# An attention and mixture-of-experts layer: query tiles loaded over sixteen units in place of the last three, and two shared-expert results kept in SBUF

## The chip, the cores and the metric

The kernel runs on one core of a Trainium2 chip. The metric is the device time of one execution in microseconds (us), as the median of several runs. Engines are written as the profile has them: PE (TensorE, matrix products), PEld (its weight loads), DVE (VectorE), ACT (ScalarE), POOL (GpSimd) and SP (SyncE, which here only issues DMAs). "SPq" and "POOLq" are the instruction queues of SP and POOL.

## The reference

The input x is 4 batches of 2048 tokens of 256 numbers. Two halves follow each other, each with a layernorm before and after and an added residual.

```python
x = x + _layernorm(attn(_layernorm(x)))
x = x + _layernorm(ffn(_layernorm(x)))
```

The attention has 16 heads of 16 numbers. Each head projects a token's query and key to one number (q_proj, k_proj), and a query i gathers the values v_j with a triangular weight (the reference does so by sorting and prefix sums):

```
out_i = sum_j max(0, 1 - |q_i - k_j| / b_h) * v_j / 2048
```

The feed-forward part has one shared expert for every token (512 hidden numbers, scaled by a sigmoid gate) and 64 routed experts. It works on all 8192 tokens at once: each token goes to the 8 experts with the largest softmax probability, an expert keeps its first 128 rows, and the results, weighted, are added to the shared expert's:

```python
w, idx = jax.lax.top_k(probs, TOP_K)          # TOP_K = 8, of 64
y = out_e[e_flat, slot] * w_flat[:, None]     # experts' rows, weighted
y = jnp.where((pos < CAPACITY)[:, None], y, 0)   # CAPACITY = 128
return y.reshape(T, TOP_K, H).sum(axis=1) + shared
```

## The kernel before

**The attention loop** takes most of the time. It has 1024 units, 256 for each batch. A unit is one head and one key tile of 128 keys, against all 2048 queries of the batch. Units come in phases of 64: 16 key tiles s, and for each of them the phase's 4 heads j. So a unit is written (s, j), and the last key tile's units are (15, 0) to (15, 3).

`score(t)` forms the weights of unit t in a tile `hat` of 128 x 2048 numbers. ScalarE computes |q - k| from the head's query tile `qb` (line 1558; for some units VectorE does it in two instructions, lines 1553 and 1555), and VectorE cuts it to the triangle in place (line 1562). `product(t)` (line 1588) multiplies on PE with the values, in four pieces of 512 queries that belong to the units t, t-1, t-2 and t-3. Only when the last piece is issued, three units later, is the hat tile given back.

`load_q(n)` (line 1539) loads the query tile of head n: one number for each query, broadcast over the 128 partitions, in two DMAs, 512 KB in SBUF. Query tiles, hat tiles and a few others share 13 large buffers, handed out strictly in turn: `take` pops the buffer that was given back longest ago, `give` appends one. A query tile is given back when its head's last score (s = 15) has read it. For the next phase's four heads the kernel calls `load_q` at (11, 0), (15, 0), (15, 1) and (15, 2). A load waits on SP until its buffer is free, and all other DMAs that SP issues wait behind it.

**Background work.** All else (projections, layernorms, shared expert, routing, routed experts) is a list of tasks in a planner, `Background`. A task names its engine, a cost, the tasks it depends on, and buffers that it takes and gives back: "slot" (10 tiles of 128 x 1024), "big" (the 13 large ones), "bank" (PSUM) and "v". Every unit calls `step()`, which emits the tasks whose turn has come by the planner's own clock (costs, the lags between engines, and a task's `lat` where it has one). The plan is made when the kernel is built, so it fixes each engine's order; on the chip an engine waits wherever the data isn't there. After the loop `drain()` plans the rest, the tail, in the same way.

**The feed-forward part by halves.** Tokens are counted in 16 chunks of 512, four for each batch. Chunks 0 to 7 (batches 0 and 1) have their experts' sums early. For batches 2 and 3 the routed experts are worked through in the tail as 15 items. An item gathers its rows (`L1217`, POOL), has its products on PE (`L1229`, `L1240`), scales them on VectorE (`L1254`) and adds them into `y_d` in memory by an indirect accumulating DMA, the scatter (`L1258`, POOL). Item i gathers only after item i-5 has scattered. There are two such targets, `y_d[1]` and `y_d[2]` for the two halves of a pair of experts; a token's result is the sum of both and of the shared expert.

The shared expert's results of batch 2 (`shared(c)` in `finish`) are stored into `y_d[1]` (line 619), so that the scatters add onto them, and once more into a second tensor, `ysh_d` (line 624), for a seldom-taken repeat at the end, which isn't run with these inputs. All scatters wait for all of these stores (`ys = stored[2]`). The shared results of batch 3 stay in SBUF.

**The final stage.** `final(c)` forms a chunk's output: a load of 512 KB from `y_d` (line 1281), for chunks 8 to 15 a second load and an add on VectorE (line 1288); for chunks 12 to 15 an add of the shared rows from SBUF (`more`, line 1314); then the layernorm: statistics (1292), means and variances (1296, 1297), a power of -1/2 on POOL (1298), shift (1301, 1302), scaling on ScalarE (1307). Last, an accumulating DMA adds the rows to the output tensor in memory (1321, POOL), where the attention's result already lies. Chunks 0 to 7 run beside the items; 8 to 15 wait for the last scatter.

**Zeros.** `y_d[2]` and batch 3's part of `y_d[1]` are set to zero by twelve stores of 512 KB from one large buffer of zeros, every eight units of batch 1 (lines 1649 to 1657).

Of the kernel before, what the change touches and what calls it, by code (L numbers as in the profile page):

```python
# [11 lines left out]
ALU = mybir.AluOpType  # L12
# [128 lines left out]
def sandwich_kernel(ctx: ExitStack, tc: tile.TileContext, x_in, wqT, bq, wkT, bk, wvT, bv, wprojT, log_bw,  # L141
                    gate_w, sgate_w, sgu_w, sd_w, egu_w, ed_w, out):
    nc = tc.nc
    P = 128
    B, T, F = x_in.shape
# [3 lines left out]
    NT = T // P  # L149
    CH = 4  # L150
    NCH = NT // CH
    CT = CH * P
# [28 lines left out]
    NE = 2  # L181
# [4 lines left out]
    ysh_d = dram.tile([T, F], F32, name="ysh_d")  # L186
# [10 lines left out]
    def yrows(r0, n, j=0):  # L197

        p, r = part(r0)
        return rows(y_d[p + j], r, n)  # L200
# [22 lines left out]
    def rows(ap, r0, n):  # L223
        return ap[r0:r0 + n * P, :].rearrange("(n p) f -> p n f", p=P)

    with ExitStack() as ph:
# [14 lines left out]
        def make(tag):  # L241
# [12 lines left out]
                return bigp.tile([P, T], F32, tag=tag, name=f"{tag}_{uid[0]}")  # L254
            return ps.tile([P, BK], F32, tag=tag, name=f"{tag}_{uid[0]}")

        NES, ess = 4, []
        bg = Background(make)
        bg.free["slot"] = [(f"s{i}", 0) for i in range(NSLOT)]
# [73 lines left out]
        def chunkview(t_):  # L333
            return t_[:, :CH * F].rearrange("p (n f) -> p n f", n=CH)
# [121 lines left out]
        def finish(b, after=()):  # L456

            env = {}
# [102 lines left out]
            def shared(c):  # L561
# [32 lines left out]
                for i2 in range(2):  # L594
# [15 lines left out]
                    if i2 == 0:  # L610
# [5 lines left out]
                    a = bg.add("pe", 1.07, lambda f=mmy: f(3), [a], put=acts if i2 == 1 else [], env=env)  # L616
                    yy += [e0, bg.add("dve", 0.45, lambda f=evy: f(1), [a, e0], put=[py], env=env)]
                free_act = a
                free_ys = bg.add("sp", 1.0, lambda ys=ys, r0=r0: nc.sync.dma_start(yrows(r0, CH, 0),
                                                                                   chunkview(env[ys])),  # L620
                                 yy, put=[] if b == NE else [ys], env=env)
# [645 lines left out]
        def final(env, c, deps, more=None, xd=(), tag=""):  # L1267


            yy, sm, xx = ("yy" + tag, c), ("sm" + tag, c), ("xx" + tag, c)  # L1270
            r0 = c * CT
            two = c >= NE * NCH
            S = lambda o, n: env[sm][:, o:o + n]
            st = lambda i: S(i * 6, 6)
            mv = lambda: S(CH * 6, 2 * CH).rearrange("p (n a) -> p n a", a=2)
            rs, sh = lambda: S(CH * 8, CH), lambda: S(CH * 9, CH)
            yv = lambda i: env[yy][:, i * CH * F:(i + 1) * CH * F]
            y3 = lambda: yv(0).rearrange("p (n f) -> p n f", n=CH)

            def load(i):  # L1280
                nc.sync.dma_start(yv(i).rearrange("p (n f) -> p n f", n=CH), yrows(r0, CH, i))
            l0 = l1 = bg.add("sp", 1.0, lambda: load(0), deps, get={yy: "big" if two else "slot"}, env=env)
            if two:
                l1 = bg.add("sp", 1.0, lambda: load(1), [l0])
            put = [yy]

            def add():
                nc.vector.tensor_tensor(yv(0), yv(0), yv(1), ALU.add)

            def stats():  # L1290
                for i in range(CH):
                    nc.vector.bn_stats(st(i), y3()[:, i, :])

            def scale():
                for i in range(CH):
                    nc.vector.bn_aggr(mv()[:, i, :], st(i))
                nc.vector.tensor_scalar_add(rs(), mv()[:, :, 1], EPS)
                nc.gpsimd.tensor_tensor(out=rs(), in0=rs(), in1=mhalf, op=ALU.pow)  # L1298

            def shift():  # L1300
                nc.vector.tensor_tensor(sh(), mv()[:, :, 0], rs(), ALU.mult)
                nc.vector.scalar_tensor_tensor(out=sh(), in0=sh(), scalar=-1.0, in1=cv[:, c * CH:(c + 1) * CH],
                                               op0=ALU.mult, op1=ALU.subtract)

            def norm():
                for i in range(CH):
                    nc.scalar.activation(y3()[:, i, :], y3()[:, i, :], AF.Identity, bias=sh()[:, i:i + 1],  # L1307
                                         scale=rs()[:, i:i + 1])
            a = bg.add("dve", 0.0, lambda: None, [l0, l1], get={sm: "v"}, env=env)
            put.append(sm)  # L1310
            if two:
                a = bg.add("dve", 1.25, add, [a])
            if more is not None:
                a = bg.add("dve", 1.25, lambda: nc.vector.tensor_tensor(yv(0), yv(0), more(), ALU.add),
                           [a] + list(xd))
            a = bg.add("dve", 1.7, stats, [a])
            a = bg.add("dve", 0.7, scale, [a], lat=2)
            a = bg.add("dve", 0.35, shift, [a])
            a = bg.add("act", 2.1, norm, [a])
            if not tag:  # L1320
                return bg.add("pool", 2.0, lambda: nc.gpsimd.dma_start(rows(of, r0, CH), y3(), accum_op=ALU.add), [a],  # L1321
                              put=put, env=env)
            lx = bg.add("sp", 1.0, lambda: nc.sync.dma_start(chunkview(env[xx]), rows(x1_d, r0 - NE * T, CH)), [l1],
                        get={xx: "slot"}, env=env)
            a = bg.add("dve", 1.25, lambda: nc.vector.tensor_tensor(yv(0), yv(0), env[xx][:, :CH * F], ALU.add), [a, lx])
            return bg.add("sp", 1.0, lambda: nc.sync.dma_start(rows(of, r0, CH), y3()), [a], put=put + [xx], env=env)
# [207 lines left out]
        def load_q(n):  # L1534

            b, g, p, s, j, h = unit(n // 4 * UP + n % 4)
            qb[n] = take(f"qb_{b}_{h}")
            for m in range(KF):
                nc.sync.dma_start(qb[n][0][:, m * HK * P:(m + 1) * HK * P],
                                  zq_d[b][m, h:h + 1, :].to_broadcast([P, HK * P]))  # L1540
# [58 lines left out]
        with tc.manual_schedule():  # L1599
            for n in range(4):  # L1600
                load_q(n)
            for t in range(B * NU + 5):
# [46 lines left out]
                if b == 0 and u == 200:  # L1649
                    zt_, z_tag = take("zeros")  # L1650
                    nc.gpsimd.memset(zt_[:, :CH * F], 0.0)
                    zfill = [(1, c) for c in range(NE * NCH, B * NCH)] + [(0, c) for c in range((B - 1) * NCH, B * NCH)]
                if b == 1 and u % 8 == 4 and zfill:
                    i, c = zfill.pop(0)
                    nc.sync.dma_start(yrows(c * CT, CH, i), chunkview(zt_))
# [9 lines left out]
                    bg.flush(last[b + 1]["v"][s:s + 1])  # L1665
                    nc.sync.dma_start(vtile(b + 1, s).rearrange("p a w -> p (a w)"), v_d[b + 1][s])
                if n + 4 < B * H:
                    if s == 11 and j == 0:
                        if ph_ == NU // UP - 1:
                            bg.flush(last[b + 1]["z"])  # L1670
                        if b == 0 and ph_ == 1:
                            bg.flush(last[0])
                        load_q(n + 4)
                    if s == NT - 1 and j < 3:
                        load_q(n + 5 + j)
                was = bg.spent["dve"]
                bg.step()
                spare[0] -= bg.spent["dve"] - was
# [35 lines left out]
            def second(deps, tag):  # L1714
                for c in range(NE * NCH, B * NCH):
                    l = c - (B - 1) * NCH
                    if l < 0:
                        final(env, c, deps, tag=tag)
                    else:
                        final(env, c, deps, lambda l=l: env["ys", l // 2][:, l % 2 * CH * F:(l % 2 + 1) * CH * F],  # L1720
                              outs[2 * l:2 * l + 2], tag)
# [68 lines left out]
```

## Time and profile before

| what | us |
|---|---|
| median of 3 runs | 2340.97 (2337.17 to 2342.14) |
| the profiled execution's own time | 2339.91 |
| its span | 2338.0 |
| ACT busy (84% of the span) | 1966.8 |
| DVE busy (85%) | 1996.1 |
| PE busy (84%) | 1952.5 |
| POOL busy (21%) | 490.4 |
| score on ACT, L1558, 959 x 1.995 | 1837.3 |
| cut on DVE, L1562, 1024 x 1.223 | 1230.3 |
| products on PE, L1588, 8192 x 0.620 | 1115.3 |

The loop's scores start at 64.3 us and end at 2033.6 us; the tail takes the rest. In a group's row the last part is the idle time of the engine just before these instructions, with what ended most of it. In a timeline's row the first two numbers are the start and the length in us, then come engine, line, operation, output and inputs, a count, and in brackets the idle time before it and its releaser. A list of waits gives the total in us, the number of waits and the longest.

### The profile page before, as it was taken

The numbers are of one execution on the slowest core, as the hardware profiler recorded it, in microseconds if no ns is written. First come the engines' busy times: TensorE is split into PE (matmuls) and PEld (weight loads), VectorE is DVE, ScalarE is ACT, GpSimd is POOL, SyncE is SP. The second block draws the span as 40 slices with busy tenths as digits, with TensorE's granted clock in tenths as the row PEclk, the third lists the DMA queues.
The fourth block names the chain that finished last, engine by engine and source line by source line (L and its number), as shares of the span: only waits on it lengthen the run. The fifth ranks groups of instructions, "written<-read, shape, count | busy, mean of one in ns | idle before, by whom it ended". The sixth has DMA issues, their size and how long they took to land. (4 is left out here: it accounts for less than half of the span.)

```text
span 2338.0 us, 32679 instructions
## 1 busy us (share of the span) xinstructions
PE 1952.5 (84%) x12552; PEld 687.2 (29%) x12552; DVE 1996.1 (85%) x3102; ACT 1966.8 (84%) x1269; POOL 490.4 (21%) x339
## 2 busy tenths in 40 slices
PE   7898979888799899677899887878888889987783
PEld 4332323222223222112222222223332223364342
DVE  4799999898999889999989998989999979886335
ACT  2899999898999998999999998989999989742213
POOL 1001010010120000003200003446553234442463
PEclk9999999999999999989999998999999999988897
DMA  4243534427351202142302014465544243355758
GB/s 127 91 133 120 184 103 153 151 88 264 117 162 64 91 19 70 37 147 69 112 19 81 28 54 122 114 186 151 174 121 136 57 134 90 102 177 147 177 124 197
DMA packets 195078, 274.32 MB, mean 117 GB/s; under 512 B 24833, under 2 KB 165505, under 8 KB 194145
## 3 DMA queue, kind: packets, MB, share of 16 engines
q1 hardware_dynamic: 165680, 235.33, 31.2%
q0 software_dynamic: 23824, 31.70, 8.3%
q10 hardware_dynamic: 5408, 5.11, 0.7%
q8 instruction: 101, 1.65, 0.3%
q14 instruction: 65, 0.52, 0.1%
HBM read 189.18 MB, written 82.90 MB: 116 GB/s over the span
## 5 line engine op out<-in xcount | busy, mean ns | idle before, releaser
L1558 ACT ACTIVATE hat<-qb,nk 128x2048 f32<-128x2048 f32 x959 | 1837.3, 1995 | 112.8 <-DMA qb<-zq_d 57.5
L1588 PE MATMUL pa<-hat,v 128*32 128x512 f32 x8192 | 1115.3, 620 | 284.4 <-DVE hat L1562 272.3
L1562 DVE TENSOR_SCALAR hat<-hat 128x2048 f32<-128x2048 f32 x1024 | 1230.3, 1223 | 97.2 <-ACT hat L1558 91.3
L1588 PEld LDWEIGHTS pa<-hat,v 128*32 128x32 f32 x8192 | 186.2, 110 | 900.0 <-DVE hat L1562 652.6
L1066 POOL DMA_INDIRECT y_d<-s,ix x64 | 147.8, 2309 | 286.7 <-DVE s L1064 145.4
L573 PE MATMUL k<-s,sgu 128*128 128x512 f32 x352 | 198.4, 651 | 0.0
L1041 POOL DMA_INDIRECT s<-tab_d,ix x64 | 106.0, 1657 | 327.6 <-DMA qb<-zq_d 259.0
L499 POOL TENSOR_TENSOR rsc<-rsc,mhalf 128x2 f32<-128x2 f32 x24 | 53.4, 2225 | 521.2 <-DVE rsc L498 521.0
L602 PE MATMUL k<-sd,s 128*128 128x256 f32 x384 | 113.7, 428 | 16.9 <-DVE s L589 7.4
L442 PE MATMUL k<-s,s 128*32 128x512 f32 x768 | 102.4, 592 | 0.0
L602 PEld LDWEIGHTS k<-sd,s 128*128 128x128 f32 x384 | 72.2, 205 | 86.4 <-issue 47.8
L573 PEld LDWEIGHTS k<-s,sgu 128*128 128x128 f32 x352 | 54.8, 192 | 136.3 <-issue 121.2
L305 POOL TENSOR_TENSOR rsa<-rsa,mhalf 128x4 f32<-128x4 f32 x16 | 30.8, 1925 | 290.9 <-DVE rsa L304 285.6
L1553 DVE TENSOR_SCALAR hat<-qb,nk 128x2048 f32<-128x2048 f32 x65 | 83.1, 1279 | 0.1
L1555 DVE TENSOR_SCALAR hat<-hat 128x2048 int32<-128x2048 int32 x65 | 79.9, 1229 | 2.2
L350 PE MATMUL k<-h,s 128*128 128x256 f32 x256 | 73.0, 413 | 0.0
L713 DVE MAX8 codes<-scT 128x8 f32<-128x1152 f32 (+2 forms) x48 | 63.4, 1321 | 0.2
L350 PEld LDWEIGHTS k<-h,s 128*128 128x128 f32 x256 | 45.4, 195 | 54.4 <-issue 48.6
L715 DVE MATCH_REPLACE8 scT<-codes,scT 128x1152 f32<-128x1152 f32 (+2 forms) x44 | 57.6, 1310 | 0.0
L607 DVE TENSOR_SCALAR s<-k,gt 128x256 f32<-128x256 f32 x48 | 22.8, 480 | 36.5 <-PE k L602 32.0
L442 PEld LDWEIGHTS k<-s,s 128*32 128x32 f32 x768 | 31.6, 138 | 54.0 <-issue 53.2
L1258 POOL DMA_INDIRECT y_d<-v,ix x28 | 39.9, 1426 | 23.5 <-DMA y_d<-s 7.9
(319 smaller groups left out, 1643.2 us busy)
## 6 DMA issues: line engine op xcount, KB each, us to landing
qb<-zq_d SPq DMA_DIRECT2D x128, 512.0 KB, 5.5
s<-m_d SPq DMA_DIRECT2D x48, 512.0 KB, 4.8
s<-_attn_hidden_states_dram SPq DMA_DIRECT2D x28, 512.0 KB, 5.5
v_d<-h SPq DMA_DIRECT2D x48, 192.0 KB, 2.6
v<-v_d SPq DMA_DIRECT2D x48, 192.0 KB, 2.5
h<-fn_expert_gate_up_w_dram SPq DMA_DIRECT2D x32, 256.0 KB, 3.5
s<-fn_expert_gate_up_w_dram SPq DMA_DIRECT2D x32, 256.0 KB, 2.8
b<-y_d SPq DMA_DIRECT2D x16, 512.0 KB, 9.3
```

Of the source, the lines that this page charges most:

```text
L350: nc.tensor.matmul(env[pk][:, i * F:(i + 1) * F], lhsT=xv[:, k, o:o + P], rhs=wv[:, k, :], start=(k == 0), stop=(k == KF - 1))
L442: nc.tensor.matmul(env[pz][c * CR:(c + 1) * CR, :], lhsT=xv[:, r, :], rhs=env[mp][:, k * 2 * F:(k + 1) * 2 * F], start=(r == 0 and k == 0) ...
L573: nc.tensor.matmul(env[p_], lhsT=sgu[:, k, o:o + P], rhs=featview(env[xT])[:, k, :], start=(k == 0), stop=(k == KF - 1))
L602: nc.tensor.matmul(env[py][:, i * F:(i + 1) * F], lhsT=env[acts[f // 2]][:, o:o + P], rhs=sd[:, f, :], start=(f == 0), stop=(f == NI - 1))
L713: a = bg.add("dve", 1.25, lambda c8=c8: nc.vector.max(out=c8, in_=scT[:, :w]), ev + [a])
L1041: g = bg.add("pool", 1.3, lambda: nc.gpsimd.indirect_dma_start(out=xg(), out_offset=None, in_=tab_d[half][:, :], in_offset=bass.IndirectOf ...
L1066: s = bg.add("pool", 1.9, lambda: nc.gpsimd.indirect_dma_start(out=y_d[half][:, :], out_offset=bass.IndirectOffsetOnAxis(ap=iv(), axis=0), ...
L1553: nc.vector.tensor_scalar(ht, qb[n][0], k, None, ALU.add)
L1555: nc.vector.tensor_scalar(hi, hi, 0x7fffffff, None, ALU.bitwise_and)
L1558: nc.scalar.activation(ht, qb[n][0], AF.Abs, bias=k)
L1562: nc.vector.tensor_scalar(ht, ht, 1.0, 1.0, ALU.min, ALU.subtract)
L1588: nc.tensor.matmul(pa[k, c][32 * j:32 * j + 32, :], lhsT=vt[b, s].rearrange("p a w -> p (a w)")[:, h // 2 * VW + p * D:h // 2 * VW + p * D ...
```

## The change

1. The query tiles of the next phase's heads are loaded at (12, 0), (13, 2), (15, 0) and (15, 1), in place of (11, 0), (15, 0), (15, 1) and (15, 2). Two flushes of the planner that stand with the first load move with it.
2. For chunks 2 and 3 of batch 2 (`LATE`) the shared rows are no longer stored into `y_d[1]`. They are stored into `ysh_d` only, and their slots stay held (`held`) until `final` has added them from SBUF. The scatters therefore wait for the stores of chunks 0 and 1 only. The two parts of `y_d[1]` are set to zero ahead instead: fourteen stores of zeros.
3. In `final`, where shared rows are added from SBUF (chunks 10 to 15 now), the second load becomes an accumulating DMA on POOL onto the first load's tile, which waits until the first has landed, and the add on VectorE goes.
4. The first load of chunks 0 to 7 has a planned latency of 9.

```diff
+        LATE, held = (2, 3), {}
...
+                if b == NE and c in LATE:
+                    held[c] = env, ys, yy
+                    free_ys = bg.add("sp", 1.0, lambda ys=ys, c=c: nc.sync.dma_start(rows(ysh_d, c * CT, CH),
+                                                                                    chunkview(env[ys])), yy)
+                    return
...
-            l0 = l1 = bg.add("sp", 1.0, lambda: load(0), deps, get={yy: "big" if two else "slot"}, env=env)
-            if two:
+            l0 = l1 = bg.add("sp", 1.0, lambda: load(0), deps, get={yy: "big" if two else "slot"}, env=env,
+                             lat=None if two else 9)
+            onto = two and more is not None and not tag
+            if onto:
+                l1 = bg.add("pool", 1.3, lambda: nc.gpsimd.dma_start(y3(), yrows(r0, CH, 1), accum_op=ALU.add), [l0], lat=4)
+            elif two:
                 l1 = bg.add("sp", 1.0, lambda: load(1), [l0])
...
-            if two:
+            if two and not onto:
                 a = bg.add("dve", 1.25, add, [a])
...
-                    zfill = [(1, c) for c in range(NE * NCH, B * NCH)] + [(0, c) for c in range((B - 1) * NCH, B * NCH)]
+                    zfill = [(1, c) for c in range(NE * NCH, B * NCH)] + [(0, c) for c in [NE * NCH + i for i in LATE] + list(range((B - 1) * NCH, B * NCH))]
...
-                    if s == 11 and j == 0:
+                    if s == 12 and j == 0:
...
-                    if s == NT - 1 and j < 3:
-                        load_q(n + 5 + j)
+                    if (s, j) in ((13, 2), (NT - 1, 0), (NT - 1, 1)):
+                        load_q(n + 5 + [(13, 2), (NT - 1, 0), (NT - 1, 1)].index((s, j)))
...
-                    if l < 0:
+                    if l < 0 and c - NE * NCH in held and not tag:
+                        e_, y_, d_ = held[c - NE * NCH]
+                        f_ = final(env, c, deps, lambda e_=e_, y_=y_: e_[y_][:, :CH * F], d_)
+                        bg.add("act", 0.0, lambda: None, [f_], put=[y_], env=e_)
+                    elif l < 0:
                         final(env, c, deps, tag=tag)
```

## The prediction

> **What bounds the kernel now.** First the busy time of the engines by stretches of the span: the 1024 units of the attention loop with what lies ahead of the tail, the tail up to 2204, the stretch of scatters, the final stage.
>
> ```profile
> core 0: us, PE busy (x) PEld busy (x) DVE busy (x) ACT busy (x) POOL busy (x), PEclk, DMA share, GB/s
> 64.00:2034.00 1970.00, 1684.59 (x11323) 525.11 (x11327) 1798.16 (x2415) 1871.45 (x1082) 356.49 (x195) 0.97 0.36 110
> 2034.00:2204.00 170.00, 131.96 (x509) 84.67 (x503) 112.21 (x410) 50.15 (x97) 53.96 (x56) 0.83 0.60 156
> 2204.00:2273.30 69.30, 58.75 (x269) 29.37 (x270) 23.79 (x73) 9.51 (x23) 50.02 (x38) 1.00 0.61 135
> 2273.30:2338.00 64.70, 28.98 (x89) 18.13 (x87) 33.60 (x104) 21.88 (x44) 20.67 (x16) 0.73 0.88 197
> ```
>
> To 2034 ScalarE is busy 95% of the time: its idle time is the loop's loss. The list of what ScalarE waited for says how much there is to win:
>
> ```profile
> ACT hat L1558 <- DMA qb<-zq_d: 57.5, 18, 24.5
> ACT hat L1558 <- PE pa L1588: 49.6, 52, 3.1
> ```
>
> The first line is a late query tile, the second a buffer that a product hadn't given back. Of the 57.5 us, 29.4 (24.5, 1.1 and 3.8) lie at the loop's start, on loads that the change leaves alone; 28.1 are left, in 15 waits. One of them on the timelines of SP and ScalarE, at a phase's end:
>
> ```profile
> 1522.60 3.75 SPq L1539 DMA_DIRECT2D qb<-zq_d  x6
> ...
> 1531.06 2.00 ACT L1558 ACTIVATE hat<-qb,nk 128x2048 f32<-128x2048 f32 x1 [4.64 <-DMA qb<-zq_d]
> 1535.29 2.00 ACT L1558 ACTIVATE hat<-qb,nk 128x2048 f32<-128x2048 f32 x1 [2.06 <-DMA qb<-zq_d]
> 1538.51 3.90 ACT L1558 ACTIVATE hat<-qb,nk 128x2048 f32<-128x2048 f32 x2 [1.22 <-DMA qb<-zq_d]
> ```
>
> Three tiles (six DMAs) are asked for at 1522.6, 1523.6 and 1524.5 and land at 1531.1, 1535.3 and 1538.5: a burst, each tile some 3.7 us behind the last.
>
> After 2204 the work hangs on POOL and SP. POOL's and SP's timelines:
>
> ```profile
> 2163.48 0.46 SPq L619 DMA_DIRECT2D y_d<-s  x1
> 2167.21 1.02 POOL L1298 TENSOR_TENSOR v<-v,mhalf 128x4 f32<-128x4 f32 x1 [10.02 <-DVE v L1297]
> 2200.98 0.36 SPq L619 DMA_DIRECT2D y_d<-s  x1
> 2204.55 1.65 POOL L1258 DMA_INDIRECT y_d<-v,ix  x1 [7.89 <-DMA y_d<-s]
> ...
> 2271.87 1.40 POOL L1258 DMA_INDIRECT y_d<-v,ix  x1 [0.30 <-issue]
> 2273.32 27.26 SPq L1281 DMA_DIRECT2D b<-y_d  x16
> ```
>
> No scatter of the last experts starts until the store of shared chunk 3 (2200.98) has landed; the 28 scatters then run nearly back to back, and the 16 loads of the final stage start at once behind the last. In that stage a chunk's square root on POOL (L1298) comes 5.46 us after the one before (2288.39 to 2321.15, six steps), and DMA is the other limit:
>
> ```profile
> q0 software_dynamic: 4304, 4.26, 45.6%
> q1 hardware_dynamic: 8448, 8.39, 41.5%
> ```
>
> These are the queues of the window 2273 to 2338 (packets, MB, share of 16 engines). q0 is eight accumulating output stores: 0.456 x 65 / 8 = 3.7 us of all engines for 512 KB. q1 is 16 plain loads: 0.415 x 65 / 16 = 1.7 us each.
>
> **The change part by part.** The sum is made against the profiled execution, 2339.91 us (span 2338.0 and 1.9 around it), 1.06 under the median.
>
> *Query loads.* A unit takes 1970/1024 = 1.92 us. Head 1's load moves from the last key tile to six units earlier, 11.5 us: more than its longest wait (4.6), so its waits go (5.95 us over the loop). Head 2's goes one unit up and has one load less ahead of it in the burst: 1.9 + 3.2 us (usual spacing of a burst). Head 3's is issued one unit earlier, but its buffer comes from a product at about the time that the old one did, so only the shorter burst helps: 3 to 5 us. In the phase shown, without stalls the tiles would be wanted at 1526.4, 1528.4 and 1530.4, so they are 4.6, 6.9 and 8.1 us late; after, 0, 1.8 and at most 3.0 to 5, so 3 to 5 of its 7.9 us stay. This is the worst phase; in the others the sums are 1 to 5.5 us and nearly all goes. I take -21 of 28.1; ends 0 (SP still waits for the buffer) and -28. The first load, to key tile 12 from 11, keeps four key tiles of 7.7 us: no price against the slowest landing, 12.7 us. What hides it is the 16 units; without them it costs 3 us a phase.
>
> *Buffers.* All large tiles share 13 buffers, handed out in turn. The earlier load holds one from key tile 13 to 15, so more scores take a buffer that a product gave back only just before. From ScalarE's timeline, the distance in units between the two: today 394 scores at distance 6 (1.9 us of waits for the product), 395 at 5 (12.7), 77 at 4 (11.7; 0.151 each), 39 at 3 (20.3; 0.52 each). Played through with the new order: 424 at 6, 311 at 5, 102 at 4, 54 at 3, six at 2 (no row; 1 us each, twice the row of 3). That is 2.1 + 10.0 + 15.4 + 28.1 + 6 = 61.6 against 46.6: +15. Part of today's waits are themselves followed by query stalls that vanish, so ScalarE runs closer on the products: not under 0 all the same, as no score gets an earlier buffer in those units; the upper end, all lateness of the products shifted by one unit, +17.5. Taken +13. VectorE and PE (85% and 84%) follow in the shadow of ScalarE, with unchanged orders.
>
> *Zero stores.* Two more stores of 512 KB in batch 1, at a DMA share of 0.36 and off any path; the zeros' buffer is held 16 units longer, at most 16 x 0.12 = 2 us of buffer waits. Taken 0; the cover is the idle 64% of DMA, and without it each costs its 1.7 us.
>
> *Late shared rows.* The two stores of batch 2's chunks 2 and 3 into the scatter's target go; the scatters wait only for chunks 0 and 1 (stored by 2082). The two slots stay held up to the end: the orders of PE, VectorE, ScalarE and POOL are the same up to 2156, so this costs nothing in the loop. In the new order POOL's first scatter stands behind the square root at 2167.21, so it can start at 2168, not 2204.55; behind it are now four square roots and their output stores (waits of ScalarE and VectorE) that came before, and they hold the scatters up. Its operand is the bound above: the first expert product (L1254) comes at 2188.96 today. POOL's own work: 28 x (1.40 + 0.30) + 10 x 1.31 = 61 us, in the 68.7 that the stretch takes; with 13 us of square roots and stores in between, from 2168: 2242; from 2190, with half of those: 2258; plus today's 7.5 of waits, 2250 to 2265. PE sets another floor: 89 us of matmuls between 2156.7 and the last scatter, so not before 2246. Taken 2257 for 2273: -16; ends -27 and 0.
>
> *Final stage.* Six of eight chunks lose an add on VectorE (L1288, 1.23 us), but six need the add of the shared rows (L1314) in its place, two of them newly. Today one add is already in the shadow of the square root and L1314 is not; after, L1314 takes the shadow, and the chain is 4.7 us a chunk: 6 x 0.76 = -4.6. Against it six plain loads (1.7 us each) become accumulating DMAs on POOL, each waiting for its first load to land. If one costs the 3.7 us of an accumulating store: 6 x 2.0 = +12 of 16-engine time, a stage of 10 x 1.7 + 14 x 3.7 = 69 for 56.6, which at 64.7 us leaves little room; if it costs a plain load's, 0. Their issue is 1.32 us each on POOL (L1321), which has 5.46 - 1.6 - 1.3 = 2.5 us free per chunk. Taken: nearer to the store (the same queue, the same size), +8; with the adds +3. Ends -5 and +12.
>
> Sum: -21 + 13 - 16 + 3 = -21; 2339.91 - 21 + 1.06 = **2320 us**.
>
> A rule that speaks against it: the Trainium skill, SBUF — State Buffer, section "SBUF: two separate sides", says that GpSimd can't write a DMA's descriptors while VectorE runs certain two-port operations, and (under "A bandwidth-pool intuition that's wrong") gives 620 ns alone against 3100 ns for such a DMA. By that factor of five each accumulate would take 6.6 us of POOL and the time would be 2348, an estimate from that page. The rows bear out less: see the fourth rival.
>
> **The rivals.**
> *The scatters gain little.* Their rows come from experts whose weights and products are themselves late: the last products (L1254) are at 2265.5 and 2268.1, 4 us ahead of the last scatters. If PE's pace and not POOL's decided, the end of the scatters moves 6 us, and the stage loses its +6: -8 - 6 + 6, **2333**. For it: PE 58.75 of 69.3 us; against: product buffers are freed by the scatters, so PE's pace follows POOL's.
> *The loads stay late.* The buffers, not the issue, set when tiles land: main loop +6 (0 to -9 for the loads, +15), tail -13: **2334**. For it: distances fall to 2 just where loads are issued. Against: in the burst shown the issues are 1 us apart and the landings 4.
> *Slower: the accumulates become the bound.* If they go one after another at x us, the stage is 10 x 1.7 + 14x + 9 of lead. The gains ahead of it are 24 us, so it decides from a stage over 65 + 24 + 4.7 = 94, x = 4.9. At the shortest landing of such a store, 5.7 us: 106 us, +41, **2358**. For it: 14 such DMAs in one queue, each but eight behind a load; against: today eight overlap at 3.7, with landings of 8.5.
> *POOL's issue is held out by VectorE.* An indirect DMA's issue takes 2.31 us in the loop (L1066), 1.40 in the tail (L1258). At the worst row, 3.41: 1.6 + 1.3 + 3.4 = 6.3 us a chunk, over 5.46: +5, and the -4.6 is lost: **2330**. Against: output stores take 1.29 to 1.40 us in the stage itself.
>
> **How the numbers follow.** Forecast 0.50 (own range 2304 to 2330); scatters gain little 0.17; loads late 0.10; slower 0.18; POOL held out 0.05. A measurement of this kernel tells 0.2% (4.7 us) from no change. Forecast 0.48 faster, 0.02 same; the second and third 0.19 faster, 0.07 same, 0.01 slower; slower 0.18; the last 0.05 faster: **0.72, 0.09, 0.19**. Range **2302 to 2348**: it leaves out most of the slower case and little below.
>
> **What would show it.** Waits of L1558 for qb near 36 us in all; for PE near 63; hats ending 8 us earlier than 2034; the first L1258 before 2190 and the last by 2262 with no wait for y_d<-s; the final stage 62 to 72 us, ten L1281 loads, q0 over half of the DMA time. Wrong: PE waits over 75, or scatters ending past 2270, or POOL waiting on its own queue's accumulates in the final stage.

## The result

The changed kernel takes 2319.91 us (median of 4 runs, 2317.5 to 2322.5) against 2339.85 (median of 4). The two medians are 19.9 us apart; the ratio on record is 0.9926, with a 95% interval of 0.9904 to 0.9948, and timed again beside other kernels it stood at 0.9929 (0.9913 to 0.9946). By these ratios it is about 17 us faster. The median that was forecast (2320) was met; most of the terms it was summed from were not, as the stretches show.

The profile after, in four stretches like those of before: the loop, the next 170 us of the tail, the rest of it up to the end of the last scatter, the final stage. (The first scatter now lies in the second stretch.) The columns are the stretch, its length, the busy time of each engine with its instructions, the granted clock, the share of the DMA engines and GB/s.

```profile
core 0: us, PE busy (x) PEld busy (x) DVE busy (x) ACT busy (x) POOL busy (x), PEclk, DMA share, GB/s
62.70:2015.00 1952.30, 1671.92 (x11323) 521.29 (x11327) 1796.32 (x2414) 1871.36 (x1082) 350.19 (x195) 0.98 0.37 112
2015.00:2185.40 170.40, 136.24 (x540) 81.73 (x542) 115.01 (x416) 50.11 (x98) 69.14 (x67) 0.85 0.61 162
2185.40:2249.40 64.00, 49.51 (x226) 28.86 (x226) 21.34 (x66) 8.85 (x21) 36.17 (x27) 0.92 0.57 113
2249.40:2320.70 71.30, 35.17 (x102) 21.13 (x100) 29.70 (x101) 22.35 (x45) 28.41 (x23) 0.74 0.94 179
```

ScalarE's busy time in the loop is the same (1871), so the loop's shortening, from 1969.3 (64.3 to 2033.6) to 1952.3 us, is idle time of ScalarE that went. From the loop's end to the last scatter's end it was 239.7 us and is 234.4; this stretch is called the scatter stretch below. The final stage was 64.7 and is 71.3. Together with a start that is 1.6 us earlier: -17.0 - 5.3 + 6.6 - 1.6 = -17.3 us of span.

What ScalarE waited for, in the list of its waits (total us, number, longest):

```profile
ACT hat L1568 <- PE pa L1598: 52.9, 53, 2.6
ACT hat L1568 <- DMA qb<-zq_d: 35.3, 7, 23.9
```

The first row is a wait for a buffer that a product still holds, the second a wait for a late query tile. The late query tiles fell from 57.5 to 35.3 us, and 28.8 of that is the start, which the change doesn't touch. The waits for a product's buffer rose by only 3.3 us, from 49.6.

The tail on POOL's and SP's timelines, the first and the eleventh scatter among the rows:

```profile
2153.43 1.67 POOL L1264 DMA_INDIRECT y_d<-v,ix  x1 [2.62 <-DVE v L1260]
...
2189.33 1.50 POOL L1264 DMA_INDIRECT y_d<-v,ix  x1 [4.56 <-DVE v L1257]
...
2190.40 0.37 SPq L1287 DMA_DIRECT2D s<-y_d  x1
...
2198.18 1.04 POOL L1308 TENSOR_TENSOR v<-v,mhalf 128x4 f32<-128x4 f32 x1 [5.63 <-DVE v L1307]
...
2206.60 1.51 POOL L1264 DMA_INDIRECT y_d<-v,ix  x1 [2.12 <-DVE v L1240]
...
2248.00 1.41 POOL L1264 DMA_INDIRECT y_d<-v,ix  x1 [0.30 <-issue]
...
2249.36 11.73 SPq L1287 DMA_DIRECT2D b<-y_d  x10
```

The first scatter now waits for its own operand and not for a store. Counted from the loop's end it starts at 138.4 us instead of 171.0, 32.6 us earlier. But from the first to the eleventh scatter it is 53.2 us, where it was 29.8, and the other 18 take 42.8, where they took 38.9. So 27.3 of the 32.6 us are given back before the last scatter. What SP waited for in the tail, in the kernel before and in the changed one, is loads of the final stage's first chunks that need a slot which an output store still reads:

```profile
SPq L1281 <- DMA out_dram<-s: 25.3, 3, 12.8
```
```profile
SPq L1287 <- DMA out_dram<-s: 49.8, 4, 21.4
```

The longest of the new waits, 21.4 us, ends with chunk 7's load at 2190.40.

The DMA queues in the final stage (window 2249 to 2321; first the busy share of the DMA engines in tenths and the GB/s in 40 slices, then packets, MB and share of 16 engines), and the waits that go with them, on VectorE's timeline and in the list of waits:

```profile
DMA  4779999999999999999999899809909999009900
GB/s 52 253 175 357 365 353 349 350 350 331 215 200 196 199 197 197 197 197 197 199 196 158 84 195 191 131 0 117 172 11 94 207 147 143 9 10 118 177 1 0
q0 software_dynamic: 7472, 7.41, 69.1%
q1 hardware_dynamic: 5280, 5.24, 23.5%
```
```profile
2271.35 1.23 DVE L1324 TENSOR_TENSOR b<-b,s 128x1024 f32<-128x1024 f32 x1 [8.39 <-DMA b<-y_d]
...
2282.78 0.69 DVE L929 TENSOR_TENSOR b<-b,k 128x512 f32<-128x512 f32 x1 [7.00 <-ACT b L925]
...
ACT b L925 <- DMA out_dram<-b: 7.1, 1, 7.1
```

The fourteen accumulating DMAs take 0.691 x 72 / 14 = 3.6 us of all engines each, the ten plain loads 0.235 x 72 / 10 = 1.7. Eight of the fourteen are the output stores, which took 3.7 us before; by difference the six into SBUF took some 3.4 each, about what one into memory costs. Chunk 10's accumulate, issued at 2261.55, lets VectorE's add start only at 2271.35. VectorE then waits for L925 on ScalarE, which itself waited 7.1 us for a buffer of an output store (`out_dram<-b`, the last row): that store stands in the same queue q0 as the accumulates.

### The profile page after: what moved, and what is told of

Its sections match the earlier page's. It is cut to its first block, busy times and chain, and to the rows that moved or that the text cites. A ratio compares the mean times of both kernels' runs of the same rounds, so it can differ in the third digit from the quotient of the medians.

```text
span 2320.7 us, 32679 instructions
## 1 busy us (share of the span) xinstructions
PE 1941.7 (84%) x12552; PEld 682.8 (29%) x12552; DVE 1990.7 (86%) x3098; ACT 1966.5 (85%) x1269; POOL 493.2 (21%) x345
## 5 line engine op out<-in xcount | busy, mean ns | idle before, releaser
L1568 ACT ACTIVATE hat<-qb,nk 128x2048 f32<-128x2048 f32 x959 | 1837.3, 1996 | 96.2 <-PE pa L1598 52.9
L1072 POOL DMA_INDIRECT y_d<-s,ix x64 | 143.0, 2235 | 289.1 <-DVE s L1070 139.3
L603 PE MATMUL k<-sd,s 128*128 128x256 f32 x368 | 105.3, 415 | 12.2 <-DVE s L608 11.2
L603 PEld LDWEIGHTS k<-sd,s 128*128 128x128 f32 x368 | 67.1, 199 | 79.2 <-issue 46.9
L351 PEld LDWEIGHTS k<-h,s 128*128 128x128 f32 x256 | 45.1, 194 | 54.5 <-issue 49.8
L721 DVE MATCH_REPLACE8 scT<-codes,scT 128x1152 f32<-128x1152 f32 (+2 forms) x44 | 57.5, 1308 | 0.0
L608 DVE TENSOR_SCALAR s<-k,gt 128x256 f32<-128x256 f32 x46 | 21.8, 479 | 38.1 <-PE k L603 29.8
```

Of the source, the lines that this page charges most:

```text
L351: nc.tensor.matmul(env[pk][:, i * F:(i + 1) * F], lhsT=xv[:, k, o:o + P], rhs=wv[:, k, :], start=(k == 0), stop=(k == KF - 1))
L603: nc.tensor.matmul(env[py][:, i * F:(i + 1) * F], lhsT=env[acts[f // 2]][:, o:o + P], rhs=sd[:, f, :], start=(f == 0), stop=(f == NI - 1))
L1072: s = bg.add("pool", 1.9, lambda: nc.gpsimd.indirect_dma_start(out=y_d[half][:, :], out_offset=bass.IndirectOffsetOnAxis(ap=iv(), axis=0), ...
L1568: nc.scalar.activation(ht, qb[n][0], AF.Abs, bias=k)
```

## Experiments

Each kernel was timed beside the kernel before. Times by stretches come from each kernel's own profiled execution; that of identical loops differs by up to 7 us (the changed kernel's loop took 1952.3 us in one profile and 1958.3 in the other), so a single loop length is read with that margin. The scatter stretch has a margin too: in the six profiles of kernels that have the changed kernel's instructions there it is 230.1 to 234.4 us, and in the two with those of the kernel before 239.7 and 243.5.

### The two halves of the change

The new load places alone, in the kernel before:

```diff
-                    if s == 11 and j == 0:
+                    if s == 12 and j == 0:
...
-                    if s == NT - 1 and j < 3:
-                        load_q(n + 5 + j)
+                    if (s, j) in ((13, 2), (NT - 1, 0), (NT - 1, 1)):
+                        load_q(n + 5 + [(13, 2), (NT - 1, 0), (NT - 1, 1)].index((s, j)))
```

> The kernel before with the new places of the query loads alone. Theory A (from the two traces: the loop became 18.6 us shorter, the tail 1.3 us longer): 2340 - 18 = 2322 us; the waits of ScalarE for query tiles fall from 57.5 to about 35, those for a product's buffer stay within 5 us of 49.6; scatters, final stage and their distances to the loop's end as before (239.7 and 64.7 us). Theory B (the prediction's sizes): buffer waits 13 us up, 2340 - 8 = 2332 us. Rival: part of the loop's gain comes from the tail's edits (fewer stores, other background work): 2326 to 2335.

Measured: ratio 0.9953 (0.9934 to 0.9971), -11 us. The list of ScalarE's waits of this kernel:

```profile
ACT hat L1558 <- PE pa L1588: 53.6, 55, 3.4
ACT hat L1558 <- DMA qb<-zq_d: 35.4, 7, 24.2
```

Its loop takes 1953.2 us, the stretch to the last scatter's end 243.5 and the final stage 64.0. So the loop's gain, -16, belongs to the load places alone, and not to the tail's edits; by the loop theory A holds. Of the whole time, the -11 lies between A's -18 and B's -8: this execution's scatter stretch is 4 us longer than in the kernel before, with the same instructions.

The changed kernel with the old load places (the same lines the other way round):

> The changed kernel with the old places of the query loads: the held shared rows, the accumulating loads and the planned latency alone. Theory A (from the traces: scatters end 5.3 us earlier against the loop's end, final stage 6.6 us longer): 2340 + 1 = 2341 us, loop as before (ends near 2033). Theory B (the prediction's sizes, scatters 16 us earlier, stage 3 longer): 2327 us. If the tail's gain depends on where the loop leaves the queues, something between.

Measured: ratio 0.9994 (0.9980 to 1.0007). Loop 1968.7 us, to the last scatter's end 230.9, final stage 71.2. The tail's edits move work (-8.7 and +6.5 us) and gain next to nothing: the prediction's -13 for them is out of the interval. And the changed kernel again, beside other kernels:

> The changed kernel itself, on the chip of the three kernels beside it. All theories: ratio 0.9926 to the kernel before; if it stands nearer to 0.9947, the sum of the two halves' ratios (0.9953 and 0.9994), the halves add up.

Measured: 0.9929 (0.9913 to 0.9946). The product of the halves, 0.9947, is 0.2% above it and at the edge of its interval. By the expectation's measure the halves don't quite add up; whether they help each other by some 4 us is left open.

### What a query tile's buffer costs

Other places for the loads, with the order of instructions on PE, VectorE, ScalarE and POOL unchanged:

```diff
-                    if s == 12 and j == 0:
+                    if (s, j) == (13, 2):
...
-                    if (s, j) in ((13, 2), (NT - 1, 0), (NT - 1, 1)):
+                    if (s, j) in ((14, 2), (15, 0), (15, 1)):
```

> The changed kernel with the loads at (13,2), (14,2), (15,0), (15,1); the orders of PE, VectorE, ScalarE and POOL are unchanged. By distance counts (2: 6, 3: 42, 4: 52, 5: 309, 6: 488 scores) and the changed kernel's measured waits per score (0.95, 0.39, 0.14, 0.027, 0.002 us) the buffer waits would be 38.6 us, 11.6 less than 50.2. Theory A (the waits of a phase aren't additive: a score that waits moves all later ones away from the products): 2 to 5 us less, query waits as they are (35): 2315 to 2318 us. Theory B (additive): 2308 us. Rival: the later first load costs as much in query waits: 2320 or more.

Measured: ratio 0.9965 (0.9950 to 0.9979), slower than the changed kernel. ScalarE's waits:

```profile
ACT hat L1568 <- PE pa L1598: 57.7, 47, 7.6
ACT hat L1568 <- DMA qb<-zq_d: 40.6, 10, 24.3
```

Theory B falls: fewer scores stand at short distances, and the buffer waits didn't fall by 11.6. They seem not to have fallen at all, but one wait of 7.6 us among them (unit 831, at 1660 us) has another cause: PE had itself stood 4.0 us for a gather (`s<-tab_d,ix`), for a reason that stays open, and the changed kernel has under 1 us of buffer waits in that phase. Without it they are some 3 us less than in the changed kernel's first profile, as theory A had it. The rival has 5 us of the loss (query waits 40.6). One load every four units instead:

```diff
-                    if (s, j) in ((13, 2), (NT - 1, 0), (NT - 1, 1)):
+                    if (s, j) in ((13, 0), (14, 0), (15, 0)):
```

> The changed kernel with the loads at (12,0), (13,0), (14,0), (15,0), one every four units; engine orders unchanged. Counts by distance 2: 26, 3: 81, 4: 74, 5: 289, 6: 424. Theory B (additive): buffer waits 75 us, +25, and the 6.5 us of query waits after the first phase go: 2338 us. Theory A (shared within a phase, a quarter of the additive price): +6 - 6: 2317 to 2323 us.

Measured: ratio 1.0037 (1.0023 to 1.0051).

```profile
ACT hat L1568 <- PE pa L1598: 85.1, 73, 3.6
ACT hat L1568 <- DMA qb<-zq_d: 29.5, 3, 24.3
```

No query tile is late after the start, and the buffers cost 32 us more than in the changed kernel: the kernel is slower than before. Here theory A's quarter price falls, and B's +25 is near. What fits both kernels, on the average of their phases, is the smallest distance that a phase reaches. By phase, from the timeline of ScalarE and the order in which buffers are handed out: the kernel before reaches 3 in every phase and pays 46.6 / 15 = 3.1 us a phase; the changed kernel reaches 2 in three phases, which pay 7.6, 5.5 and 5.8 us (3.7, 5.6 and 3.1 in the kernel before), and 3 in the other twelve, 31.0 / 12 = 2.6 us; even loads reach 2 in fourteen phases, (80.7 - 4.4) / 14 = 5.5 us. (These leave the first phase out.) Single phases spread widely about these means: from 0 to 6 us at a smallest distance of 3, from under 1 to over 12 with even loads. The reason offered is that a score that waits moves all later scores of the phase away from their products, so that only a still smaller distance makes one wait again; this is argued, not shown. To test the means, one buffer less:

```diff
-        NBIG = 13
+        NBIG = 12
```

> The changed kernel with 12 large buffers in place of 13: every distance between a product's release and the next use falls by one (2: 52, 3: 109, 4: 316, 5: 435 scores), the engines' orders in the loop stay. Theory B (each score pays by its distance: 0.95, 0.39, 0.14, 0.027 us): 147 us of buffer waits for 50, the loop 95 us longer. Theory C (formed after the two kernels with other load places: a phase pays once, for the smallest distance that it reaches, about one unit of 1.92 us for each step of it; the changed kernel reaches 2 in six phases and 3 in the others, this one 2 or less in all): buffer waits 66 to 80 us, the loop 17 to 30 us longer.

Measured: ratio 1.0219 (1.0191 to 1.0248).

```profile
ACT hat L1568 <- PE pa L1598: 105.9, 114, 3.3
ACT hat L1568 <- DMA cx_d<-ct: 17.0, 6, 3.5
```

102 us of buffer waits after the first phase, 6.8 us a phase, with the smallest distance 2 in every phase. (The second row is a buffer that the store of `ct` still reads; it was 5.1 us in the changed kernel.) The 102 is under B's 147 and over C's 66 to 80. C's sum took six phases of the changed kernel for 2, where there are three; with 5.5 to 6.3 us a phase at 2, as measured above, it would have been 82 to 95. So the smallest distance explains most of the price, but a phase that stays at short distances for long (52 scores at 2 and 109 at 3, against 26 and 81 with even loads) pays more. The loop is 2019.7 us long, 61 to 67 longer than the changed kernel's two.

### What holds the scatters

Half of the shared expert's first matmuls of batch 3 left out, all else in its order:

```diff
-                        for k in range(KF):
-                            nc.tensor.matmul(env[p_], lhsT=sgu[:, k, o:o + P], rhs=fv(c)[:, k, :],
-                                             start=(k == 0), stop=(k == KF - 1))
+                        for k in range(1):
+                            nc.tensor.matmul(env[p_], lhsT=sgu[:, k, o:o + P], rhs=fv(c)[:, k, :],
+                                             start=True, stop=True)
```

> The changed kernel with half of batch 3's shared first matmuls left out (one of the two K halves; so batch 3's shared part is not the reference's), all other instructions in the same order. In the stretch of scatters they take 14 + 14.5 us of PE, 16 behind it. Theory A (PE's pace sets the end of the scatters): they end 8 to 14 us earlier against the loop's end, 2306 to 2312 us. Rival (POOL's and the loads' waits set it): within 3 us, 2316 to 2321 us.

Measured: ratio 0.9944 (0.9929 to 0.9958); scatter stretch 234.1 us, against 234.4 and 232.5 in the changed kernel's two profiles: theory A falls. PE's work alone is not the bound, though the test is weaker than meant: from the first scatter to the last PE's busy time fell only from 77.0 to 71.5 us, at a granted clock of 0.79 in the first ten scatters where the changed kernel had 0.90. The 13 second scatters of the pairs left out:

```diff
             def scatter(j):
+                if j == 1:
+                    return
                 nc.gpsimd.indirect_dma_start(
```

> The changed kernel with 13 of the 28 scatters left out (the second of each pair of experts, so its rows are missing in the output), all other instructions in the same order. If POOL's pace sets the end of the scatters: 13 x 1.72 = 22 us less of POOL's work, the last scatter 12 to 20 us earlier against the loop's end. If the items' chain through PE and VectorE sets it: under 5 us.

Measured: 2320.25 us in a single run; scatter stretch 225.2 us, 7 to 9 less than in the changed kernel's two profiles and 5 less than in any with the same instructions. That lies between the two cases of the expectation. The changed kernel's last 18 scatters, and the same stretch of this kernel, as busy times:

```profile
2206.60:2249.40 42.80, 36.97 (x174) 19.92 (x169) 14.15 (x43) 5.69 (x15) 29.71 (x22) 0.96 0.51 101
```
```profile
2208.00:2245.50 37.50, 34.77 (x173) 18.73 (x170) 14.40 (x44) 5.69 (x15) 16.91 (x13) 1.00 0.42 97
```

Leaving out half of POOL's scatters shortens this part by 5.3 us only; PE is then busy 93% of it (34.77 of 37.50). Two bounds lie close together: PE with 37 us, and POOL with 18 x 1.7 + 4 x 1.3 = 35.8 us with its issue times. So half_shared and half_scatter, which each lift one of them, could show little; that is an argument from these sums. This is the second part of the scatters; the first ten scatters (53.2 us for 29.8) are another matter. Two kernels bear on them. Chunks 6 and 7 of the final stage in large buffers:

```diff
-            l0 = l1 = bg.add("sp", 1.0, lambda: load(0), deps, get={yy: "big" if two else "slot"}, env=env,
+            l0 = l1 = bg.add("sp", 1.0, lambda: load(0), deps, get={yy: "big" if two or (c >= 6 and not tag) else "slot"}, env=env,
```

> The changed kernel with chunks 6 and 7 of the final stage in large buffers in place of slots, so that their loads don't wait for one of the two slots fewer. Theory A: in the changed kernel the loads of chunks 6 and 7 stand on SP until 2161 and 2190, with expert weights queued behind them, and POOL waits for chunk 7's statistics to 2198; without that the scatters end 5 to 12 us earlier: 2308 to 2315 us. Rival: PE's pace sets the end of the scatters (49.5 of 64 us busy): 2318 to 2322 us.

Measured: ratio 0.9940 (0.9916 to 0.9963); first scatter to eleventh 46.1 us, but the first starts 145.7 us after the loop's end and not 138.4; scatter stretch 233.9. Theory A falls, and the time lies where the rival had it. Chunk 7 is then done before the first scatter, but the kernel is no clean test: the two chunks take large buffers that the experts' weights had. Loads of weights now wait for a buffer that a product still reads, 20.6 us on SP in the first row (in the changed kernel such waits come to 0.4 us). ScalarE, whose queue issues half of these loads, stands 13.1 us before an activation of shared chunk 3, just ahead of the first scatter:

```profile
SPq L1204 <- PE k L1256: 20.6, 2, 12.1
...
2156.49 0.60 ACT L588 ACTIVATE s<-pa 128x512 f32<-128x512 f32 x1 [13.06 <-DMA b<-L_ffn_expert_down_w_dram]
```

Then shared chunk 3's matmuls, activations and products left out, with the order of the rest unchanged (`quiet` adds a task that does nothing for this chunk; the same for its product on VectorE):

```diff
+                skip = b == NE and c == 3
...
+                    return add_(eng, cost, (lambda: None) if skip and eng in ("pe", "act") else fn, *a, **k)
...
-nc.vector.tensor_scalar(chunkview(env[ys])[:, t, :], env[py][:, i * F:(i + 1) * F],
+nc.vector.tensor_scalar(chunkview(env[ys])[:, t, :], sd[:, 0, :] if skip else env[py][:, i * F:(i + 1) * F],
```

> The changed kernel with the matmuls, activations and products of batch 2's shared chunk 3 left out (its shared rows are then the gate times a weight row, so not the reference's); all other instructions in the same order. Theory A (in the changed kernel the items' instructions stand behind this chunk's on PE and VectorE, which wait for slots and for chunk 7's late load, so the wait of the scatters has only moved into these queues): the scatters end 8 to 15 us earlier against the loop's end, 2305 to 2313 us. Rival (POOL's own pace, 28 scatters and 10 gathers, sets it): within 4 us, 2316 to 2323 us.

Measured: ratio 0.9930 (0.9905 to 0.9955); scatter stretch 229.9 us, 2.6 to 4.5 less than in the changed kernel's two profiles and hardly outside the 230.1 to 234.4 of all with the same instructions. So theory A fails in its size, and the size is the rival's. The rival's reason, POOL's own pace, isn't the whole of it in the first ten scatters: in the changed kernel POOL is busy 32.2 of their 53.2 us. This kernel's lines show what stands there:

```profile
2198.05 0.37 SPq L1292 DMA_DIRECT2D s<-y_d  x1
...
2202.71 1.41 DVE L1307 BATCH_NORM_STATS2 v<-s 128x6 f32<-128x256 f32 x4 [9.25 <-DMA s<-y_d]
...
2204.95 1.08 POOL L1313 TENSOR_TENSOR v<-v,mhalf 128x4 f32<-128x4 f32 x1 [8.85 <-DVE v L1312]
2206.23 1.08 POOL L1228 DMA_INDIRECT v<-tab_d,ix  x1 [0.20 <-issue]
...
2206.58 1.09 ACT L1322 ACTIVATE s<-s,v 128x256 f32<-128x256 f32 x2 [21.09 <-DVE v L1317]
...
2209.74 0.66 PE L1234 MATMUL pa<-ident,v 128*128 128x128 f32 x2 [12.53 <-DMA v<-tab_d,ix]
```

With chunk 3's work gone, chunk 7's load still goes out only at 2198, VectorE stands 9.3 us before its statistics, POOL 8.9 us before the chunk's square root, and the items' instructions stand behind that: on VectorE and ScalarE directly, on PE through a gather that POOL issues only behind the square root (2206.23). In the changed kernel shared chunk 3 stands in the same chain:

```profile
2195.81 1.40 DVE L1302 BATCH_NORM_STATS2 v<-s 128x6 f32<-128x256 f32 x4 [5.91 <-DMA s<-y_d]
...
2197.65 2.07 PE L603 MATMUL pa<-sd,s 128*128 128x256 f32 x4 [7.39 <-DVE s L608]
```

Chunk 7's load, issued at 2190.40 after its 21.4 us for a slot, holds VectorE; the scaling of shared chunk 3's rows (L608) stands behind it there, PE waits 7.4 us for that, and the items' matmuls for the eleventh scatter come after it on PE. Without chunk 3's work the late load still holds the items by itself. No kernel had the load early and all large buffers free, or more slots, so that this chain costs the 23 us is argued and not shown.

### The final stage

The second load of chunks 10 to 15 as a plain load again:

```diff
-            onto = two and more is not None and not tag
+            onto = False
```

> The changed kernel with the second load of chunks 10 to 15 again a plain load on SP and the add on VectorE; the orders up to the last scatter are those of the changed kernel. Theory A: the accumulating loads set the longer final stage (queue q0 takes 69% of the DMA engines there, and the store of chunk 8 lands behind four of them), so it falls from 71.3 to 64 to 66 us: 2314 us. Rival: the stage is longer because it starts with more of PE's shared-expert work undone (35 us of it in place of 29): 2319 to 2323 us, and with the two adds a chunk even longer.

Measured: ratio 0.9922 (0.9902 to 0.9942). The last row of its stretches and its DMA queues in the stage:

```profile
2252.10:2317.90 65.80, 32.07 (x102) 20.00 (x100) 36.56 (x107) 22.23 (x45) 23.52 (x17) 0.76 0.86 194
```
```profile
q0 software_dynamic: 4304, 4.26, 44.3%
q1 hardware_dynamic: 8448, 8.39, 40.3%
```

The stage falls from 71.3 to 65.8 us, as theory A had it, with PE's work in it nearly the same (32 us against 35): the accumulating loads are what lengthened it. (Every profile with them has 70.7 us or more in the stage, every one without 64.0 to 65.9.) The whole time should then be 5.5 us (0.24%) lower; the ratio is 0.04% to 0.07% lower, and 0.24% is within the intervals, so the timing neither shows nor excludes it (its profiled loop took 1955.6 us). The same without the planned latency of 9:

```diff
-            l0 = l1 = bg.add("sp", 1.0, lambda: load(0), deps, get={yy: "big" if two else "slot"}, env=env,
-                             lat=None if two else 9)
+            l0 = l1 = bg.add("sp", 1.0, lambda: load(0), deps, get={yy: "big" if two else "slot"}, env=env)
```

> The changed kernel with plain second loads for all chunks and without the planned latency of 9 for chunks 0 to 7, so that only the held shared rows and the query loads are left of the change. The plan of the tail differs: POOL has the square roots and stores of chunks 3 to 7 otherwise placed among the scatters. Theory A (the accumulating loads lengthen the final stage by 5.6 us, the order before it costs little): 2313 to 2318 us. If the planned latency is what brings the scatters forward, they end 5 us or more later against the loop's end: 2320 to 2326 us.

Measured: ratio 0.9945 (0.9928 to 0.9963). Final stage 65.9 us, and scatter stretch 236.8, against 231.9 with the latency (and 230.1 to 234.4 in the six profiles named at the start of the experiments). The first scatter starts at 2175.7 instead of 2158.3. The time, 2323.9 us, lies where the expectation had it if the planned latency brings the scatters forward. So the latency, for which the prediction's sum has no term, goes with 2 to 7 us of the scatters' gain; without it the held rows bring 3 us of the 239.7, or 7 of the 243.5.

## Why the prediction was right, and where its terms were not

*Query loads, -21.* Right, in mechanism and size: 28.1 us of late tiles after the start became 6.5 and, in the second profile, 7.5, and the load places alone do it. In the phase that was worked through, 4.1 of 7.9 us stay, where 3 to 5 were forecast. (A query tile is two DMAs of 512 KB each, 1 MB in SBUF.)

*Buffers, +13.* Wrong in size: 46.6 us became 49.9 and, in the second profile, 53.2; the load places alone give 50.6. The step that failed is carrying today's price of each score over to more scores and adding up. The counts by distance were right within a few scores. The six at distance 2 cost 0.95 us each, about the 1 us assumed; the 54 at distance 3 cost 0.39 each and not 0.52, some 21 us in all where 28.1 was set down. More scores at 3 paid together what fewer had paid. That a phase pays mainly for the smallest distance it reaches, which the change lowers in three phases of fifteen, fits the means of the three kernels with other load places or fewer buffers. The loop became 17.0 and 11.0 us shorter in the changed kernel's two profiles (14 on the average of nine profiles with this loop), and not 8.

*Late shared rows, -16.* Wrong in size: -5.3 and -7.1 us in the two profiles, and -5 to -13 if all profiles with either tail are taken. The release of the first scatter was as forecast: 138.4 us after the loop's end, between the two starts named (2168 and 2190, which are 134 and 156 after it). What failed is the step from there: 61 us of POOL's own work plus 13 of roots and stores plus 7.5 of waits. The waits were not today's. Two slots are now held, the chunks' loads wait 49.8 us for slots where they waited 25.3, and chunk 7's load comes late and keeps shared chunk 3 and the items back. The prediction had named the held slots and costed them at nothing in the loop, which holds; in the tail they were not costed. That the held slots are the whole of it is read from the timelines and not tested. The first rival's 6 us for the scatters is near what happened, and its reason, PE's pace, has a part in the last 18 scatters only, where it lies beside POOL's.

*Final stage, +3.* Wrong in size: +6.6. The cost of an accumulate, 3.6 us of all engines, was at the upper end named (3.7). The six adds were to give 4.6 us back on VectorE; the chain isn't VectorE's any more, it waits for the queue of accumulates. That all fourteen stand in one queue the prediction had said; that an output store behind accumulates keeps its source buffer, for which ScalarE then waits, it had not.

*Zero stores, 0.* The kernel with the tail's edits alone has the loop of the kernel before (1968.7 and 1969.3 us): right.

So -21 + 13 - 16 + 3 = -21 stood for about -21.6, +3 to +7, -5 to -7 and +6.6, with the rest of the difference in other waits of a few us each. The sum, -13 and -17 by the two profiles' spans and -17 by the ratio, is near the forecast because the two terms that were too large have opposite signs. That is luck: of the terms that moved, only the query loads' came out as it was worked out. The signs that the prediction named tell the same: the buffer waits came to 52.9 us and not near 63, and the loop ended 18.6 us earlier and not 8, while the query waits (35.3 for 36), the first scatter before 2190, the stage of 62 to 72 us and q0's share came as named. Of the rivals, POOL held out by VectorE doesn't set the time: the accumulates' issue did take 1.3 to 2.4 us, where the output stores took 1.3 to 1.4 before, but POOL waited 24.7 us for VectorE's results (`v`) in the stage. The Trainium skill's factor of five for such a DMA beside VectorE (SBUF — State Buffer, "A bandwidth-pool intuition that's wrong") is not seen in this stage, where an accumulate's longest issue is 1.8 times its shortest.

## What to carry to other kernels

Where buffers are handed out in turn, a prefetch that holds one more makes the engine that bounds the loop wait for buffers that were given back only just before. In these kernels adding up a price for each use overstated it, and the smallest distance between release and reuse fitted the means better: spread loads so that this distance doesn't fall, and look at it before the count. A wait that is taken from one queue shows its worth only if the instructions behind it have their operands: list what each of the next ten waits for, slots above all. An accumulating DMA saves an add on an engine that may have time, and paid here with twice the DMA time and a place in the queue of all other accumulates.

## What was not expected of the hardware

An accumulating DMA into SBUF took about as much of the DMA engines as one into memory, some 3.4 us for 512 KB against 3.7, and 1.7 for a plain load; with the accumulates alone in flight the engines were full at some 197 GB/s, where the plain loads ahead of them moved 350. And the same loop took 1951.4 to 1958.6 us in nine profiled executions of eight kernels that share it: the 7 us between them are half of what the load places gained.
